# Row sums by transfers and VectorE, b2 in norm 1's shift, norm 3 on ScalarE, and all pieces in a new order

## The chip, the cores and the metric

The kernel runs on one core of one Trainium2 chip. A core has TensorE (PE in the profile; its weight loads are PEld), VectorE (DVE), ScalarE (ACT), GpSimd (POOL) and SyncE (SP), which issues transfers. Each engine takes its instructions in the order of the program; semaphores make one wait for another. Sixteen DMA engines move data. The metric is the device time in microseconds (us) of one execution.

## What is computed

32 graphs of 512 nodes with 256 features pass through two layers of masked attention with norms around them. Cut to what matters:

```python
# layer 0
allowed = (adj > 0) | (adj.swap > 0) | eye
scores  = where(allowed, (q * 32**-0.5) @ k.T, -inf)        # 8 heads of 32
x1  = layernorm1(x + (softmax(scores) @ v) @ Wo.T + bo)      # with gain and shift
ff  = relu(x1 @ W1.T + b1) @ W2.T + b2                       # 1024 hidden
x2  = layernorm(x + layernorm2(x1 + ff))                     # "norm 3" is the outer one
# layer 1
scores = where(adj == 0, -inf, q @ k.T / sqrt(32))
out = layernorm(x2 + (softmax(scores) @ v) @ Wo.T + bo)      # "norm 4"
```

## The kernel before

A graph's score matrix is held transposed, keys on the 128 partitions and queries along the row. One layer of one graph is cut into eight pieces k = 0 to 7: a group of four heads (`hg` = 0 or 1) and a block of 128 keys. For each piece, `scores` (L338) makes four matmuls of 32 rows into one PSUM tile of 128x2048, and ScalarE's exp turns it into `p` (L349). `masked` (L352) multiplies `p` by the 0/1 mask on VectorE. `product` (L356) multiplies with the values and adds over the four key blocks into `acc`; the last one is copied to `cT`. The exps aren't normalised, so their sums over all 512 keys are needed as divisors. The pool of `p` has eight buffers of 1 MB, those of the score tile and of `acc` one each, and the pool of small PSUM tiles three.

The divisors are made thus. `pair` (L374) issues an accumulating transfer p[k] += p[k+1] from GpSimd, for k = 0, 2 and 4. `fold` (L379) adds two `p` on VectorE (L381), three times a layer, so that p[2] holds the sum of the four blocks of head group 0 and p[3] that of group 1. `sums` (L392) sums over the 128 partitions: four matmuls with a block of ones, on TensorE (L402). `divide` (L410) turns blocks of 32x32 (L414), takes the reciprocal, spreads it back with another transpose (L420) and multiplies `cT` with it (L421); two small GpSimd additions keep a running total that tells at the end whether any sum left the range. For layer 1 of the last graph the sums are matmuls over all four blocks without pairs and folds.

`project` (L453) then multiplies `cT` with Wo. The norms work on quarters of 128 nodes: `residual_statistics` (L447) adds the residual to the PSUM result and takes mean and variance on VectorE; `root` (L433) forms (variance + eps)^-0.5 in two small GpSimd instructions (L436, L437); `affine` (L442) applies gain and shift on VectorE (L444, L445). Norm 3 is one VectorE instruction a quarter (L518); norm 4 is done by ScalarE (L532) with scale 1/sigma and bias -mean/sigma, which `offset` (L523) forms on VectorE. `hidden` (L472) and `mlp` (L498) are the two dense layers. `residual1` adds the row b2 to x1 for all nodes by an accumulating transfer (L169), after the transposes of x1 were taken for the hidden layer; `residual` and `residual2` add bov and norm 2's shift in the same way.

SyncE's queue loads x twice, the cast adjacency as `m0` and its transpose as `m1`, and transposes x for layer 0 by transfers (`flip`, `sort`).

Order: nothing is scheduled by a tool. The bodies of `opening`, `period` and `closing` are lists of such calls over up to five graphs in different stages, written out by hand under `manual_schedule`; each engine gets its instructions in that order. `period` runs for 29 graphs. A piece here is a method with all its engines' work: `scores` holds its exp, `out2` the addition and the statistics.

Of the kernel before, what the change touches and what calls it, by code (L numbers as in the profile page):

```python
# [9 lines left out]
F32 = mybir.dt.float32  # L10
# [8 lines left out]
EPS = 1e-5  # L19
# [8 lines left out]
def kernel(ctx: ExitStack, tc: tile.TileContext, t: dict, out: bass.AP):  # L28
# [88 lines left out]
    bo.append(spread("L1_gnn_bo"))  # L117

# [31 lines left out]
    def plain(pools: ExitStack):  # L150
# [6 lines left out]
        BEATS = ND * NQ  # L157
# [10 lines left out]
        def add_row(dst, row):  # L168
            nc.gpsimd.dma_start(out=dst, in_=row[:, None, :].to_broadcast([P, NQ, D]), accum_op=ALU.add)  # L169

        class Absent:


            def __getattr__(self, name):
                return lambda *args, **kw: None

        class Graph:


            def __init__(self, b):  # L180
                self.b = b
                self.mv, self.rs, self.pf, self.total = {}, {}, {}, {}

            def tile(self, tag, shape, dtype=F32, **kw):
                t = work.tile([P, *shape], dtype, tag=tag, name=f"{tag}_{self.b}", **kw)
                setattr(self, tag, t)
                return t


            def load(self):  # L190
                if not hasattr(self, "x"):
                    nc.sync.dma_start(out=self.tile("x", [NQ, D]), in_=x[self.b].rearrange("(c p) d -> p c d", p=P))

            def again(self):

                if not hasattr(self, "x1"):
                    nc.sync.dma_start(out=self.tile("x1", [NQ, D]), in_=x[self.b].rearrange("(c p) d -> p c d", p=P))

            def cast(self):

                if hasattr(self, "code"):
                    return
                self.code = hbm.tile([N, N], BF16, tag="code", name=f"code_{self.b}")
                nc.gpsimd.dma_start(
                    out=self.code.rearrange("(p c) k -> p (c k)", p=P),
                    in_=adj[self.b].rearrange("(p c) k -> p (c k)", p=P),
                )

            def entries(self):

                if hasattr(self, "m0"):
                    return
                nc.sync.dma_start(
                    out=self.tile("m0", [NQ, N], BF16), in_=self.code.rearrange("(c p) k -> p c k", p=P)
                )
                self.tile("m1", [NQ, N], BF16, bufs=3)
                for i in range(NQ):
                    nc.sync.dma_start_transpose(out=self.m1[:, i, :], in_=self.code[:, i * P : (i + 1) * P])

            def masks(self):  # L220

                nc.vector.tensor_tensor(self.m0, self.m0, self.m1, ALU.max)
                diagonal = self.m0.rearrange("p c (k q) -> p (c k) q", q=P)[:, :: NQ + 1, :]
                nc.vector.tensor_tensor(diagonal, diagonal, ident_b[:, None, :].to_broadcast([P, NQ, P]), ALU.max)
                nc.vector.tensor_scalar(self.m0, self.m0, 0.0, None, ALU.is_gt)
                nc.vector.tensor_scalar(self.m1, self.m1, 0.0, None, ALU.not_equal)
# [6 lines left out]
            def once(self):  # L233

                if self.b == 0:
                    value_bias(0)

            def once1(self):
                if self.b == 0:
                    value_bias(1)  # L240

            def residual(self):

                add_row(self.x1, bov[0])
                add_row(self.x, be2)

            def flip(self, n, i):


                if i == 0:
                    self.tile("v", [NQ, D])
                    self.tile("kT", [ND, N])
                if n > 0:
                    h, j = divmod(i, 2)
                    dst, src = self.flipped(n, h)[:, :, j * P : (j + 1) * P], getattr(self, f"x{n}")[:, i, :]
                    nc.sync.dma_start_transpose(out=dst, in_=src.bitcast(U16))
                elif self.b > 0:
                    src = x[self.b, i * 2 * P : (i + 1) * 2 * P, :]  # L260
                    nc.sync.dma_start_transpose(out=self.flipped(0, i), in_=src.bitcast(U16))

            def flipped(self, n, h):
                t = self.x2[:, :2, :] if n == 1 else self.v[:, 2 * h : 2 * h + 2, :]
                return t.rearrange("p c d -> p (c d)").bitcast(U16).rearrange("p (a q) -> p a q", q=2 * P)

            def sorted(self, n, h):
                t = self.x2[:, 2:, :].rearrange("p c d -> p (c d)") if n == 1 else self.kT[:, h, :]
                return t.bitcast(U16).rearrange("p (a q) -> p a q", q=2 * P)

            def sort(self, n, h):

                if n == 0 and self.b == 0:
                    return
                src, dst = self.flipped(n, h), self.sorted(n, h)
                for w in range(2):
                    for i in range(2):
                        nc.sync.dma_start(
                            out=dst[i * P // 2 : (i + 1) * P // 2, w * ND : (w + 1) * ND, :], in_=src[w::2, i::2, :]
                        )  # L280

            def join(self, n, h):
                if n == 0 and self.b == 0:

                    self.transpose(self.x, h)
                    return
                if h == 0:
                    self.tile("xT", [ND, N])
                words = self.xT.bitcast(U16).rearrange("p c (q w) -> p c q w", w=2)
                for w in range(2):  # L290
                    nc.scalar.copy(
                        words[:, :, h * 2 * P : (h + 1) * 2 * P, w], self.sorted(n, h)[:, w * ND : (w + 1) * ND, :]
                    )


            def transpose(self, src, h):

                if h == 0:
                    self.tile("xT", [ND, N])
                ps = ps_d.tile([P, ND, 2 * P], F32, tag="d", name=f"psT_{self.b}_{h}")  # L300
                for c in range(ND):
                    for j in range(2):
                        nc.tensor.transpose(
                            ps[:, c, j * P : (j + 1) * P], src[:, 2 * h + j, c * P : (c + 1) * P], ident
                        )
                nc.scalar.copy(self.xT[:, :, h * 2 * P : (h + 1) * 2 * P], ps)

            def value(self, layer, h):
                if h == 0 and layer != 0:
                    self.tile("v", [NQ, D])  # L310
                ps = ps_d.tile([P, 2, D], F32, tag="d", name=f"psV_{self.b}_{h}")
                for j in range(2):
                    at = slice((2 * h + j) * P, (2 * h + j + 1) * P)
                    for i in range(ND):
                        nc.tensor.matmul(
                            ps[:, j, :],
                            self.xT[:, i, at],
                            proj[layer][0][2][:, i, :],
                            start=(i == 0),
                            stop=(i == ND - 1),  # L320
                        )
                nc.scalar.copy(self.v[:, 2 * h : 2 * h + 2, :], ps)

            def query_key(self, layer, which, c, h=None):

                tag = ("qT", "kT")[which]
                dst = getattr(self, tag) if c or h or (which and layer == 0) else self.tile(tag, [ND, N])
                w, bias = proj[layer][0][which], proj[layer][1 + which]
                at = slice(0, N) if h is None else slice(h * 2 * P, (h + 1) * 2 * P)
                ps = ps_d.tile([P, at.stop - at.start], F32, tag="d", name=f"psQK_{self.b}_{which}_{c}_{h}")  # L330
                for i in range(ND):
                    nc.tensor.matmul(  # L332
                        ps, w[:, i, c * P : (c + 1) * P], self.xT[:, i, at], start=(i == 0), stop=(i == ND - 1)
                    )
# [3 lines left out]
            def scores(self, layer, k):  # L338
                if k == 0:
                    self.layer, self.p, self.acc = layer, {}, {}  # L340
                hg, kc = divmod(k, NQ)
                s = ps_s.tile([P, HPC, N], F32, tag="s", name=f"psS_{self.b}_{k}")
                for j in range(HPC):
                    at = slice(j * HD, (j + 1) * HD)
                    nc.tensor.matmul(  # L345
                        s[:, j, :], self.kT[at, hg, kc * P : (kc + 1) * P], self.qT[at, hg, :], start=True, stop=True
                    )
                p = work.tile([P, HPC, N], F32, tag="p", name=f"p_{self.b}_{k}", bufs=8)
                nc.scalar.activation(p, s, AF.Exp, scale=SCALE)  # L349
                self.p[k] = p  # L350

            def masked(self, layer, k):  # L352
                p, m = self.p[k], (self.m0, self.m1)[layer]
                nc.vector.tensor_tensor(p, p, m[:, k % NQ, None, :].to_broadcast([P, HPC, N]), ALU.mult)  # L354

            def product(self, k):  # L356
                hg, kc = divmod(k, NQ)
                if kc == 0:
                    self.acc[hg] = ps_a.tile([P, N], F32, tag="acc", name=f"psA_{self.b}_{hg}")
                for j in range(HPC):  # L360
                    h = hg * HPC + j
                    nc.tensor.matmul(  # L362
                        self.acc[hg][j * HD : (j + 1) * HD, :],
# [1053 lines left out]
```

## Time and profile before

| what | value |
|---|---|
| time, median of 3 runs (lowest, highest) | 3073.57 us (3073.37, 3074.45) |
| span of the profiled execution | 3072.4 us |
| HBM read and written | 89.01 MB and 33.55 MB, 40 GB/s over the span |
| DMA share of q0 (issued by GpSimd) and q1 (by SyncE) | 51.2% and 16.1% of the span |
| mean granted TensorE clock | 0.999 |
| p<-p accumulations, 1 MB each | 189, landing 7.7 us after the issue |
| kT<-v, 64 KB each | 248, landing 3.9 us after the issue |
| masking, 128x2048 | 512, 2279 ns each |
| fold, 128x2048 | 189, 2286 ns each |
| row-sum matmuls as recorded | 1072 records (two for each matmul) |

A row of a group names line, engine, operation, output and inputs by their names in the program (buffer numbers left out), shapes and count; then the busy time in us, the mean of one in ns, and the idle time of that engine just ahead of it with what ended it. In a timeline, each line has start, duration, and what ran. The share of a DMA engine is the time that its packets took; with several queues at work it can pass 1.

### The profile page before, as it was taken

How to read it: one execution, taken by the hardware profiler on the slowest of the kernel's cores; microseconds unless marked ns; L12 is line 12 of the kernel's file. 1: busy time of each engine (PE TensorE's matmuls, PEld its weight loads, DVE VectorE, ACT ScalarE, POOL GpSimd, SP SyncE). 2: the span in 40 equal slices, each digit the busy share in tenths (PEclk: the TensorE clock that was granted, in tenths of full speed). 3: DMA queues.
4: the chain of work that ended last, by engine and by line, in shares of the span. 5: the costliest groups of instructions: out<-in, count | busy, mean ns of one | idle time of the engine just before them, and what ended most of it. 6: DMA issues, size and time to landing. Idle time of an engine off the chain costs nothing. (4 is left out here: it accounts for less than half of the span.)

```text
span 3072.4 us, 44237 instructions
## 1 busy us (share of the span) xinstructions
PE 3049.0 (99%) x17218; PEld 1728.9 (56%) x17218; DVE 2648.1 (86%) x3458; ACT 1707.3 (56%) x1983; POOL 1039.0 (34%) x1254
## 2 busy tenths in 40 slices
PE   8999999999999999999999999999999999999998
PEld 4555655556555555555555555655556555555564
DVE  6798889888889888898888988889888889888887
ACT  5455565555556555565556655565555556555554
POOL 1333333433334332343323333333433334332332
PEclk9999999999999999999999999999999999999999
DMA  9876677666767666676666766667766767666543
GB/s 207 155 141 129 116 141 145 140 123 126 136 138 148 121 131 124 138 154 122 133 124 136 148 134 131 114 141 145 139 124 126 136 137 148 120 131 124 117 83 70
DMA packets 341064, 406.54 MB, mean 132 GB/s; under 512 B 149616, under 2 KB 315632, under 8 KB 316144
## 3 DMA queue, kind: packets, MB, share of 16 engines
q0 software_dynamic: 95824, 282.09, 51.2%
q1 hardware_dynamic: 245024, 121.56, 16.1%
q8 instruction: 137, 2.24, 0.3%
q14 instruction: 79, 0.65, 0.1%
HBM read 89.01 MB, written 33.55 MB: 40 GB/s over the span
## 5 line engine op out<-in xcount | busy, mean ns | idle before, releaser
L349 ACT ACTIVATE p<-psS 128x2048 f32<-128x2048 f32 x512 | 962.2, 1879 | 657.1 <-PE psS L345 655.4
L354 DVE TENSOR_TENSOR p<-p,m 128x2048 f32<-128x2048 f32 x512 | 1155.4, 2279 | 8.4 <-ACT p L349 8.2
L436 POOL TENSOR_SCALAR rs<-mv 128x2 f32<-128x2 f32 (+1 forms) x320 | 326.3, 1020 | 940.6 <-DVE mv L431 939.7
L345 PE MATMUL psS<-qT,kT 32*128 32x512 f32 x4096 | 583.9, 640 | 2.8 <-ACT p L349 1.3
L362 PE MATMUL psA<-p,v 128*32 128x512 f32 x4096 | 492.7, 598 | 0.9 <-ACT cT L372 0.7
L502 PE MATMUL psF<-w_L_gnn_W,hT 128*128 128x256 f32 x2048 | 468.5, 382 | 0.0
L481 PE MATMUL psH<-xT,w_L_gnn_W 128*128 128x256 f32 x2048 | 467.3, 384 | 0.7 <-DMA w_L_gnn_W<-in_L_gnn_W_dram 0.7
L502 PEld LDWEIGHTS psF<-w_L_gnn_W,hT 128*128 128x128 f32 x2048 | 383.8, 190 | 123.0 <-issue 76.4
L481 PEld LDWEIGHTS psH<-xT,w_L_gnn_W 128*128 128x128 f32 x2048 | 381.4, 190 | 120.3 <-issue 47.9
L381 DVE TENSOR_TENSOR p<-p,p 128x2048 f32<-128x2048 f32 x189 | 429.5, 2286 | 6.4 <-DMA p<-p 4.7
L345 PEld LDWEIGHTS psS<-qT,kT 32*128 32x128 f32 x4096 | 159.9, 182 | 300.5 <-issue 117.2
L437 POOL TENSOR_TENSOR rs<-rs,neg_half 128x2 f32<-128x2 f32 (+1 forms) x320 | 299.6, 936 | 26.8
L362 PEld LDWEIGHTS psA<-p,v 128*32 128x32 f32 x4096 | 109.9, 109 | 315.3 <-issue 234.5
L489 ACT ACTIVATE hT<-psH,c_L_gnn_b 128x256 f32<-128x256 f32 x512 | 215.2, 472 | 120.6 <-PE psH L481 117.3
L417 POOL TENSOR_TENSOR total<-total,sT 128x16 f32<-128x16 f32 x128 | 28.4, 222 | 732.0 <-DVE sT L414 732.0
L461 PE MATMUL psO<-w_L_gnn_Wo,cT 128*128 128x256 f32 x1024 | 241.0, 383 | 0.9 <-DVE cT L421 0.9
L332 PE MATMUL psQK_None<-xT,w_L_gnn_Wqkv 128*128 128x512 f32 x512 | 238.4, 598 | 2.4 <-DMA w_L_gnn_Wqkv<-in_L_gnn_Wqkv_dram 2.4
L372 ACT COPY cT<-psA 128x512 f32<-128x512 f32 x128 | 75.0, 586 | 280.7 <-PE psA L362 280.7
L377 POOL DMA_DIRECT2D p<-p x189 | 188.2, 996 | 117.8 <-PE psA L362 108.7
L449 DVE TENSOR_TENSOR y<-psF,x 128x256 f32<-128x256 f32 x128 | 53.9, 421 | 200.1 <-PE psF L502 197.6
L461 PEld LDWEIGHTS psO<-w_L_gnn_Wo,cT 128*128 128x128 f32 x1024 | 189.3, 190 | 52.0 <-DVE cT L421 23.0
L430 DVE BATCH_NORM_STATS2 st<-y 128x6 f32<-128x256 f32 x384 | 164.3, 428 | 13.1
(68 smaller groups left out, 2930.8 us busy)
## 6 DMA issues: line engine op xcount, KB each, us to landing
p<-p POOLq DMA_DIRECT2D x189, 1024.0 KB, 7.7
x<-in_x_dram SPq DMA_DIRECT2D x64, 512.0 KB, 5.1
x<-bov POOLq DMA_DIRECT2D x64, 512.0 KB, 9.2
code<-in_adj_dram POOLq DMA_DIRECT2D x32, 512.0 KB, 6.6
m<-code SPq DMA_DIRECT2D x32, 512.0 KB, 5.6
x<-s_L_gnn_ln_b POOLq DMA_DIRECT2D x32, 512.0 KB, 10.4
x<-s_L_gnn_b POOLq DMA_DIRECT2D x32, 512.0 KB, 5.4
out_dram<-x SPq DMA_DIRECT2D x32, 512.0 KB, 9.1
```

Of the source, the lines that this page charges most:

```text
L332: nc.tensor.matmul(ps, w[:, i, c * P : (c + 1) * P], self.xT[:, i, at], start=(i == 0), stop=(i == ND - 1))
L345: nc.tensor.matmul(s[:, j, :], self.kT[at, hg, kc * P : (kc + 1) * P], self.qT[at, hg, :], start=True, stop=True)
L349: nc.scalar.activation(p, s, AF.Exp, scale=SCALE)
L354: nc.vector.tensor_tensor(p, p, m[:, k % NQ, None, :].to_broadcast([P, HPC, N]), ALU.mult)
L362: nc.tensor.matmul(self.acc[hg][j * HD : (j + 1) * HD, :], self.v[:, kc, h * HD : (h + 1) * HD], self.p[k][:, j, :], start=(kc == 0), stop ...
L381: nc.vector.tensor_tensor(self.p[dst], self.p[a], self.p[b], ALU.add)
L436: nc.gpsimd.tensor_scalar(rs, self.mv[n][:, a:b, 1:2], EPS, None, ALU.add)
L437: nc.gpsimd.tensor_tensor(rs, rs, neg_half[:, a:b, None], ALU.pow)
L461: nc.tensor.matmul(ps[:, j, :], self.cT[:, k, at], wo[layer][:, k, :], start=(k == 0), stop=(k == ND - 1))
L481: nc.tensor.matmul(ps[:, j, :], w1[:, c, at], self.xT[:, c, h * 2 * P : (h + 1) * 2 * P], start=(c == 0), stop=(c == ND - 1),)
L489: nc.scalar.activation(self.hT[h][:, f + j, :], ps[:, j, :], AF.Relu, bias=b1[:, f + j : f + j + 1])
L502: nc.tensor.matmul(ps, self.hT[h][:, f, j * P : (j + 1) * P], w2[:, f, :], start=(f == 0), stop=(f == NF - 1))
```

## The change

Every piece is cut by engines: `scores` and `exp`, `hidden` and `relu`, `add`, `stats` and `aggregate`, `center` and `affine` are calls of their own, and `opening`, `period` and `closing` are new lists of these over five graphs, `period` for 26 graphs. New or different in what is computed where:

- Row sums: after the folds, two accumulating transfers from GpSimd (`halve`) add the upper 64 partitions of the sum to the lower 64, and then 32 to 32. Four transfers from SyncE (`spread`) put the four heads' 32x512 side by side on the partitions of `part`. VectorE transposes blocks of 32x32 (`blocks`) and adds 32 to one (`reduce`). Reciprocal, spreading back and the division stay. Layer 1 of the last graph keeps the matmuls.
- b2 is added to norm 1's shift once, so x1 holds it already; its effect on the hidden layer is taken from b1 (`hidden_bias`, 16 matmuls of one column, once). The transfer of `residual1` goes.
- Norm 3 is done by ScalarE like norm 4, with `offset` for its bias on VectorE.

```diff
-        def add_row(dst, row):
-            nc.gpsimd.dma_start(out=dst, in_=row[:, None, :].to_broadcast([P, NQ, D]), accum_op=ALU.add)
...
+        def hidden_bias():
+            ps = ps_d.tile([P, NF], F32, tag="d", name="psB_2")
+            for f in range(NF):
+                for c in range(ND):
+                    nc.tensor.matmul(
+                        ps[:, f : f + 1],
+                        w1[:, c, f * P : (f + 1) * P],
+                        b2_c[:, c : c + 1],
...
+            nc.vector.tensor_tensor(b1, b1, ps, ALU.subtract)
+            nc.vector.tensor_tensor(be1, be1, b2, ALU.add)
...
-            def sums(self, k, hg, first=False, last=False):
...
+            def halve(self, layer, hg, rows):
+                p = self.p(layer, 2 + hg)
+                nc.gpsimd.dma_start(out=p[:rows], in_=p[rows : 2 * rows], accum_op=ALU.add)
+
+            def spread(self, layer, hg, j):
+                part = self.at("part", (layer, hg), [N], bufs=1)
+                nc.sync.dma_start(out=part[j * HD : (j + 1) * HD, :], in_=self.p(layer, 2 + hg)[:HD, j, :])
...
+            def blocks(self, layer, hg):
+                src = self.dense("R", (1, hg), [N]) if self.final(layer) else self.at("part", (layer, hg), [N], bufs=1)
+                nc.vector.transpose(self.sT(layer, hg).rearrange("p a b -> p (a b)"), src)
+
+            def reduce(self, layer, hg):
+                if self.final(layer):
+                    nc.vector.tensor_copy(self.total(layer, hg), self.sT(layer, hg)[:, :, 0])
+                else:
+                    nc.vector.tensor_reduce(self.total(layer, hg), self.sT(layer, hg), AX.X, ALU.add)
...
-            def norm3(self, i):
-                mean, rs = self.mean(3, i), self.rs[3][:, i, :]
-                nc.vector.tensor_scalar(self.x2[:, i, :], self.y.pop(i), mean, rs, ALU.subtract, ALU.mult)
...
+            def norm(self, n, i):
+                nc.scalar.activation(
+                    self.x2[:, i, :], self.y(n, i), AF.Identity, bias=self.ms(n)[:, i, :], scale=self.rs(n)[:, i, :]
+                )
```

From the new `period`, in its order, what concerns the row sums of graph c in layer 0 and the pieces that follow roots directly (all else left out):

```python
c.fold(0, 2, 2, 0)
c.halve(0, 0, P // 2)
...
c.product(0, 4)
c.scores(0, 7)
...
c.pair(0, 4)
c.masked(0, 6)
...
c.halve(0, 0, P // 4)
c.spread(0, 0, 2)
...
c.masked(0, 7)
c.fold(0, 3, 6, 7)
c.fold(0, 3, 3, 4)
c.halve(0, 1, P // 2)
...
c.spread(0, 0, 0)
...
d.masks(0)
c.spread(0, 0, 3)
...
c.halve(0, 1, P // 4)
...
b.masked(1, 1)
...
c.spread(0, 0, 1)
...
b.masked(1, 0)
b.scores(1, 2)
b.exp(1, 2)
b.value_out(1, 0)
c.blocks(0, 0)
c.reduce(0, 0)
d.value(0, 0)
b.scores(1, 5)
b.exp(1, 5)
...
c.aggregate(1, 0)
c.root(1, 0, 2)
c.center(1, 1)
c.affine(1, 1)
...
c.aggregate(1, 2)
c.relu(0, 7)
c.root(1, 2, 4)
c.affine(1, 3)
...
c.aggregate(2, 0)
c.hidden(1, 2)
c.relu(1, 3)
c.root(2, 0, 2)
...
c.affine(2, 1)
```

The buffers of `p` are still eight. A buffer is free again when the last piece that reads it is done; for the two sums of a layer that is now the last `spread`. `part` has one buffer.

## The prediction

> **What bounds the kernel now.** I read the page first (engine shares, slices, chain), then the groups of instructions split by shape, then one steady graph in the table of windows and in the timeline of each engine, and last the waits.
>
> ```profile
> PE 3049.0 (99%) x17218; PEld 1728.9 (56%) x17218; DVE 2648.1 (86%) x3458; ACT 1707.3 (56%) x1983; POOL 1039.0 (34%) x1254
> PE   8999999999999999999999999999999999999998
> DMA  9876677666767666676666766667766767666543
> ...
> 1000.00:1095.00 95.00, 95.00 (x538) 53.92 (x537) 83.05 (x109) 53.51 (x63) 33.18 (x40) 1.00 0.69 134
> ```
>
> TensorE is busy in 3049.0 of 3072.4 us, and in the window (columns: length, then busy us of PE, PEld, DVE, ACT, POOL, clock, DMA share, GB/s) it has no gap at all. So a steady graph costs what TensorE's instructions cost. The casts of the adjacency, one a graph, start at 218.32 us and, 26 graphs later, at 2684.84 us: the period is 94.87 us. 32 periods make 3035.8 us; the 36.6 us left are filling and draining. The chain of waits covers only the last few us and bounds nothing before them. VectorE is second: 83.05 us busy in that window, and what its idle time is made of decides how much TensorE's saving is worth:
>
> ```profile
> L449 DVE TENSOR_TENSOR y<-psF,x 128x256 f32<-128x256 f32 x4 | 1.7, 422 | 6.5 <-PE psF L502 6.5
> L445 DVE SCALAR_TENSOR_TENSOR x<-cent,rs,s_L_gnn_ln_b 128x256 f32<-128x256 f32 x4 | 1.9, 485 | 1.1 <-POOL rs L437 0.9
> L445 DVE SCALAR_TENSOR_TENSOR z<-cent,rs,x 128x256 f32<-128x256 f32 x4 | 1.9, 484 | 1.2 <-POOL rs L437 0.9
> L518 DVE TENSOR_SCALAR x<-z,mv,rs 128x256 f32<-128x256 f32 x4 | 1.5, 403 | 1.1 <-POOL rs L437 1.1
> ```
>
> These are the groups of the same window (the figure after the second bar is the idle time before the group). 6.5 us go to TensorE, 2.9 us to GpSimd's roots, and 95.0 - 83.05 - 9.4 = 2.55 us are small gaps between instructions. Without the waits VectorE needs 85.6 us of a period of 94.87.
>
> What the row sums cost TensorE I take from start to start in its timeline, as busy times of neighbours overlap:
>
> ```profile
> 1014.88 1.06 PE L362 MATMUL psA<-p,v 128*32 128x512 f32 x8
> 1015.77 1.04 PE L402 MATMUL psR<-p,ones 128*32 128x512 f32 x8
> 1016.66 2.78 PE L362 MATMUL psA<-p,v 128*32 128x512 f32 x24
> ...
> 1033.53 1.06 PE L402 MATMUL psR<-p,ones 128*32 128x512 f32 x8
> 1034.42 1.04 PE L362 MATMUL psA<-p,v 128*32 128x512 f32 x8
> ...
> 1062.77 1.04 PE L402 MATMUL psR<-p,ones 128*32 128x512 f32 x8
> 1063.74 1.14 PE L345 MATMUL psS<-qT,kT 32*128 32x512 f32 x8
> ```
>
> 0.89, 0.89, 0.97, and 1.00 us for the fourth (1066.72 to 1067.72): mean 0.94, four times a graph.
>
> [...] Here every `p<-p` is in q0; in a stretch of two of them (1058 to 1060 us in the table of windows) the share is 1.02 at 209 GB/s, so some 210 GB/s fills all engines. [...]
>
> ```profile
> 1054.45 2.26 DVE L354 TENSOR_TENSOR p<-p,m 128x2048 f32<-128x2048 f32 x1
> ...
> 1054.63 2.16 POOL L436 TENSOR_SCALAR rs<-mv 128x2 f32<-128x2 f32 x1
> ```
>
> The root's first half takes 2.16 us and ends with the masking (1056.7); where VectorE waits it takes 0.35. So a slow root costs nothing by itself: VectorE is working then. [...]
>
> **The change part by part, per graph.**
>
> TensorE. The row sums leave (only the last graph's layer 1 keeps its 32 matmuls): 4 x 0.94 = -3.75 us, to 91.1. The 16 one-column matmuls of `hidden_bias` come once.
>
> VectorE. `reduce` is new, 4 a graph, 512 elements to 16. Nearest rows: the 512-element transpose at 0.71 us and multiply at 0.69; [...] I take 0.70 [...]: +2.8. Three more `offset` at 0.154: +0.5. Norm 3's four TENSOR_SCALAR at 0.403 leave: -1.6. `blocks` reads `part` in SBUF in place of PSUM; the transposes of either source take 0.70 to 0.71: 0. Masks, folds, adds and statistics keep number and shape. Sum 85.6 + 1.7 = 87.3 us.
>
> Waits of VectorE that the new order itself forces. A root as VectorE sees it is 1.3 us in the trace (aggregate ends 1016.09, next scale 1017.38). In the new stream `affine(1,3)` stands directly behind `aggregate(1,2)`, and `affine(2,1)` behind `aggregate(2,0)`: 1.3 each. `affine(1,1)` has one `center` of 0.47 before it: 0.8. `affine(2,2)` and `offset(3,2)` have 1 to 1.5 us of work before them: 0.3 each. Sum 4.0 (0 if GpSimd were instant, 7 if the roots also queue behind GpSimd's transfers): 91.3 us. Behind a waiting `affine` stand the maskings and folds, and behind those TensorE's products.
>
> ScalarE. Norm 3 adds 4 x 0.55 (row of norm 4) = 2.2 us to 53.5; exps wait for scores anyway. Hidden. Uncovered, 2.2.
>
> GpSimd. Eight accumulating `halve` at the 1.0 us of a `p<-p` issue, less b2's 1.3: 33.2 to 39.9 us of some 92. Hidden, but roots and pairs queue behind them (in the 7 above).
>
> SyncE. 16 `spread` more at about 1.0 us issue (four `kT<-v` take 4.08 us). Each waits for the halving, and the prefetches queued behind it wait too; those are wanted most of a period later. Hidden.
>
> DMA. Now 0.69 x 94.87 = 65.5 us. Halves: 4 x (0.52 + 0.26 MB) at 210 GB/s = +15. Spreads, 1.05 MB in 2 KB rows, like `kT<-v`: about +5 (2 to 10). b2's row no longer added: -2.5. Sum 83 of some 92 us, 0.90. Not the bound, but queues form. The tightest place: `halve(0,0,32)` stands behind `pair(0,4)` in GpSimd's queue, and that behind `product(0,4)`. One issue, 7.7 us landing of the pair (row `p<-p`), some 1.5 for the halving behind it, four spread issues of 1.0, landing 3.9 (row `kT<-v`): 18 us to `blocks(0,0)`. VectorE has beside it three maskings (6.7), two folds (4.5), masks (2.3), a fourth masking (2.2) and small ones (1.1): 16.8. 1.2 us of waiting stay. The buffers that `spread` holds longer: `exp(1,5)` takes that of `p(0,2)`; TensorE has 21 us (start to start) between `product(0,4)` and the end of `scores(1,5)`: covered by 3. The other three reuses have over 10 us.
>
> b2 in norm 1's shift and the removed row addition free only hidden work. The last graphs pay some latency in draining: +3.
>
> Sum: TensorE 91.1; VectorE 87.3 + 4.0 + 1.2 = 92.5. VectorE becomes the bound by a little. For 28 graphs 92.5, for four at the edges, where the table of windows shows VectorE at 31 to 35 of 40 us, 91.1; with filling and draining 36.6 + 3: 2590.0 + 364.4 + 39.6 = 2994. That is the profiled span; the median is 1.2 us above it: 2995.
>
> **Rivals.**
> (a) TensorE stays the only bound: the roots and transfers all hide. For: ordering by pieces (center apart from affine) gives room. Against: the two direct waits above. 32 x 91.1 + 39.6 = 2955.
> (b) The waits for psF stay too: half of the 6.5 us comes on top of 91.3, as mlp to norm 2 to the next transpose is a chain through both engines. 94.5: 28 x 94.5 + 404 = 3050.
> (c) Slower: the software DMA queue runs late. Place: `blocks(0,0)` at the head of VectorE, fed by pair, two halves and spread in one queue order. Price: at 0.90 load each of the four landings 1 to 1.5 us later, all of it VectorE's, as nothing there is slack: 92.5 + 4.2 = 96.7, 28 x 96.7 + 404 = 3112. It decides from 2.4 us of lag a graph on (94.9). For: the load. Against: the slices now hold stretches with a DMA share of 0.00 (1014 to 1022 us), so there is room to move into.
> (d) No change: the removed time comes back exactly, 94.8: 3072. That the change doesn't do what it says I exclude: the new program holds 32 row-sum matmuls in place of 536.
>
> **Numbers.** 0.2% is what a measurement of this kernel can tell from no change. Forecast (91.5 to 93.6 a graph, 2965 to 3025) 0.44; (a) 0.18; (b) 0.15; (c) 0.19; (d) 0.04. Faster 0.44 + 0.18 + 0.15 = 0.77, same 0.04, slower 0.19. The range leaves out most of (c) and the lowest edge of (a): 2945 to 3095.
>
> **What would show it.** Right: a period of 92 to 93 us; TensorE at 98 to 99% with small waits for VectorE; VectorE near 93% with its idle time put down to roots (4 us a graph) and `part` (1); DMA near 0.9; `reduce` at 0.6 to 0.75 us. Wrong: `blocks` waiting several us for `part` (c); long waits for psF (b); no waits of TensorE (a); exps waiting for a transfer, which I hold covered.

## The result, and the profile after

The changed kernel takes 3292.65 us (median of 4 runs, 3284.91 to 3302.06), the kernel before 3074.01 in the same comparison: ratio 1.0712, 95% interval 1.0692 to 1.0731. It is slower by 7%, and the time lies above the whole range that I gave. The profiled execution has a span of 3292.5 us.

The page of the kernel after (engine totals, DMA by slices of the span, DMA queues):

```profile
PE 3032.3 (92%) x16242; PEld 1758.3 (53%) x16242; DVE 2652.7 (81%) x3556; ACT 1760.1 (53%) x2111; POOL 1149.4 (35%) x1474
DMA  8898989998888998898988899888999888898862
q0 software_dynamic: 95056, 364.42, 65.5%
q1 hardware_dynamic: 269488, 154.63, 20.9%
```

No engine is near its span now. TensorE has given up its 99% for 92%, VectorE its 86% for 81%; only the DMA row has filled, from 6s and 7s to 8s and 9s. The casts, one a graph, lie at 334.54 and, 25 graphs later, at 2843.43 us: a period of 100.36 us. What lies outside 25 such periods (filling, draining, and seven graphs' worth of work) is 783.6 us; the kernel before has 94.86 and 701.0.

One steady graph in the table of windows, cut in two (length, busy us of PE, PEld, DVE, ACT, POOL, clock, DMA share, GB/s):

```profile
1035.00:1085.00 50.00, 49.85 (x278) 24.86 (x280) 46.69 (x62) 33.18 (x37) 17.67 (x26) 1.00 0.73 131
1085.00:1135.00 50.00, 44.19 (x234) 30.18 (x227) 36.40 (x51) 22.57 (x31) 18.80 (x22) 0.93 1.06 196
```

In the first half TensorE has no gap and the DMA engines seem to have room (0.73). In the second they are full from end to end (1.06), and TensorE loses 5.8 us. VectorE's timeline shows where (the bracket is the idle time before the instruction and what ended it):

```profile
1105.34 0.18 DVE L518 BATCH_NORM_AGGREGATE mv<-st_(2_1_7268 128x2 f32<-128x6 f32 x1
1105.56 0.48 DVE L534 SCALAR_TENSOR_TENSOR cent_(2_1_7274<-y_(2_1_7266,mv,s_L_gnn_ln_g 128x256 f32<-128x256 f32 x1
1115.20 0.71 DVE L471 STREAM_TRANSPOSE sT_(1_0_7283<-part_(1_0_7203 128x512 f32<-128x512 f32 x1 [9.16 <-DMA part_(1_0_7203<-p_(1_2_6956]
1115.95 0.69 DVE L477 TENSOR_REDUCE total_(1_0_7285<-sT_(1_0_7283 128x16 f32<-128x512 f32 x1
1116.74 0.25 DVE L480 RECIPROCAL r_(1_0_7296<-total_(1_0_7285 128x16 f32<-128x16 f32 x1
1116.91 0.36 DVE L512 TENSOR_TENSOR y_(2_0_7303<-psF,x 128x256 f32<-128x256 f32 x1
```

`blocks(1, 0)` (L471) stands at the head of VectorE's queue and waits 9.16 us for `part`. Behind it stands `add(2, 0)` (L512), which would free a PSUM tile. TensorE's timeline at that place:

```profile
1104.44 3.62 PE L571 MATMUL psF<-w_L_gnn_W,hT 128*128 128x256 f32 x16
1107.90 3.62 PE L555 MATMUL psH<-xT,w_L_gnn_W 128*128 128x256 f32 x16
1117.32 5.62 PE L555 MATMUL psH<-xT,w_L_gnn_W 128*128 128x256 f32 x16 [5.81 <-DVE y_(2_0_7303 L512]
```

`hidden` needs that tile, so TensorE stands for 5.81 us; then the same 16 matmuls take 5.62 us where they took 3.62. The window 1115 to 1120 us shows a clock of 0.50:

```profile
1115.00:1120.00 5.00, 2.68 (x6) 2.19 (x7) 3.44 (x8) 0.00 (x0) 1.34 (x4) 0.50 1.05 190
```

Cut finer, the table has 0.50 from the end of the wait (1117.3) to 1121 us, 0.90 in the next us and 1.00 from 1122 on. With the 2.0 us of slower matmuls the wait costs 7.8 us. At this place between 700 and 2300 us of the trace 15 waits for `y`, of 5.2 to 9.6 us, are each followed by 16 matmuls in 5.1 to 6.8 us.

Why `part` is late shows in the queues. GpSimd and SyncE in that stretch:

```profile
1086.57 0.88 POOL L438 DMA_DIRECT2D p_(1_2_6956<-p_(1_2_6956  x1
...
1093.73 0.88 POOL L438 DMA_DIRECT2D p_(1_2_6956<-p_(1_2_6956  x1 [2.47 <-DMA p_(1_2_6956<-p_(1_2_6956]
```

```profile
1086.38 5.98 SPq L336 DMA_TRANSPOSE v<-in_x_dram  x2
1097.85 0.69 SPq L341 DMA_DIRECT2D kT<-v  x1
1099.29 2.05 SPq L443 DMA_DIRECT2D part_(1_0_7203<-p_(1_2_6956  x2
1101.39 1.48 SPq L341 DMA_DIRECT2D kT<-v  x1
1102.91 4.46 SPq L443 DMA_DIRECT2D part_(1_0_7203<-p_(1_2_6956  x2
```

The fold ends at 1085.8; the first halving is issued at 1086.6, the second, which needs the first, at 1093.7; the spreads follow from 1099.3, and the last lands at 1115.1: 29.4 us from fold to use. VectorE comes to it 20.2 us after the fold. Transfers of that stretch by line, with KB and median us from issue to landing:

```profile
p_(1_2_6956<-p_(1_2_6956 POOLq DMA_DIRECT2D x1, 512.0 KB, 6.9
p_(1_2_6956<-p_(1_2_6956 POOLq DMA_DIRECT2D x1, 256.0 KB, 5.4
part_(1_0_7203<-p_(1_2_6956 SPq DMA_DIRECT2D x4, 64.0 KB, 6.8
v<-in_x_dram SPq DMA_TRANSPOSE x2, 8.7
```

Three readings are open at this point. Theory Q: SyncE's queue holds the spreads behind flips and sorts. Theory D: the DMA engines are full, so all lands late in any order. Theory P: the lateness costs so much only because `blocks(1, 0)` stands ahead of `add(2, 0)`. Besides, the new order might be slow by itself.

### The profile page after: what moved, and what is told of

It reads as the page before. It is cut to its first block, busy times and chain, and to the rows that moved or that the text cites. A ratio compares the mean times of both kernels' runs of the same rounds, so it can differ in the third digit from the quotient of the medians.

```text
span 3292.5 us, 43923 instructions
## 1 busy us (share of the span) xinstructions
PE 3032.3 (92%) x16242; PEld 1758.3 (53%) x16242; DVE 2652.7 (81%) x3556; ACT 1760.1 (53%) x2111; POOL 1149.4 (35%) x1474
## 4 chain that ended last, share of the span: by engine, by line
DVE 33%; PE 29%; DMA 16%; SPq 7%; issue 7%; ACT 5%; POOL 2%; DVEq 0%; POOLq 0%; ACTq 0%
SPq L443 5%; PE psF L571 4%; PE psQK_None L383 4%; PE psH L555 3%; PE psO L501 3%; PE psQK L383 3%; PE psV L371 2%; SPq L341 2%; POOL rs L524 1%; PE psT L358 1%; DVE mv L518 1%; POOL rs L523 1%; ACT x L544 1%; DVE x L541 1%; DVE cT L492 1%
## 5 line engine op out<-in xcount | busy, mean ns | idle before, releaser
L501 PEld LDWEIGHTS psO<-w_L_gnn_Wo,cT 128*128 128x128 f32 x1024 | 202.8, 202 | 84.1 <-DVE cT L492 36.6
L383 PEld LDWEIGHTS psQK_None<-xT,w_L_gnn_Wqkv 128*128 128x128 f32 x512 | 92.6, 191 | 133.8 <-issue 109.4
L371 PE MATMUL psV<-w_L_gnn_Wqkv,xT 128*128 128x256 f32 x512 | 127.4, 392 | 0.0
L358 PE MATMUL psT<-ident,x 128*128 128x128 f32 x520 | 89.6, 292 | 40.3 <-ACT x L544 33.0
L371 PE MATMUL psV<-w_L_gnn_Wv,xT 128*128 128x256 f32 x512 | 124.4, 386 | 0.0
L371 PEld LDWEIGHTS psV<-w_L_gnn_Wqkv,xT 128*128 128x128 f32 x512 | 92.2, 189 | 58.0 <-issue 25.2
L371 PEld LDWEIGHTS psV<-w_L_gnn_Wv,xT 128*128 128x128 f32 x512 | 92.5, 190 | 36.5 <-issue 26.5
L363 ACT COPY xT<-psT 128x512 f32<-128x512 f32 x130 | 75.1, 578 | 60.7 <-PE psT L358 60.7
L323 POOL DMA_DIRECT2D x<-bov x64 | 98.1, 1532 | 3.2 <-PE psT L358 2.1
L348 ACT COPY xT<-kT 128x512 uint16<-128x512 uint16 x124 | 94.2, 765 | 7.0 <-DMA kT<-v 4.7
L376 ACT COPY v<-psV 128x512 f32<-128x512 f32 x128 | 73.9, 581 | 11.7 <-PE psV L371 11.6
```

The source lines that it names most:

```text
L348: nc.scalar.copy(words[:, :, h * 2 * P : (h + 1) * 2 * P, w], self.sorted(h)[:, w * ND : (w + 1) * ND, :])
L358: nc.tensor.transpose(ps[:, c, j * P : (j + 1) * P], src[:, 2 * h + j, c * P : (c + 1) * P], ident)
L371: nc.tensor.matmul(ps[:, j, :], xT[:, i, at], proj[layer][0][2][:, i, :], start=(i == 0), stop=(i == ND - 1))
L383: nc.tensor.matmul(ps, w[:, i, c * P : (c + 1) * P], xT[:, i, at], start=(i == 0), stop=(i == ND - 1))
L501: nc.tensor.matmul(ps[:, j, :], self.cT(layer)[:, k, at], wo[layer][:, k, :], start=(k == 0), stop=(k == ND - 1))
```

## The experiments

Ratios are to the kernel before, with the 95% interval. Period and edges (what lies outside 25 periods) are worked out from the casts as above; "DMA" is the time of q0 and q1 over 32 graphs. Where a mean wait is named below, it is that of VectorE at this place over the graphs between 800 and 2500 us of the trace.

| run | ratio | period | edges | DMA, us a graph |
|---|---|---|---|---|
| kernel before | 1 | 94.86 | 701 | 64.6 |
| kernel after | 1.0712 (1.0692 to 1.0731) | 100.36 | 784 | 88.9 |
| e1 sorts behind | 1.0667 (1.0649 to 1.0685) | 99.97 | 780 | 88.3 |
| e2 blocks late | 1.0673 (1.0644 to 1.0702) | 100.38 | 781 | 88.3 |
| e3 less load | 1.0505 (1.0473 to 1.0538) | 97.98 | 784 | 82.2 |
| e4 all sums on TensorE | 1.0159 (1.0142 to 1.0176) | 95.18 | 742 | 62.9 |
| e5 biases early | 1.0650 (1.0617 to 1.0682) | 99.27 | 774 | 88.8 |
| e6 and flips late | 1.0725 (1.0686 to 1.0764) | 100.00 | 788 | 89.0 |
| e7 and blocks late | 1.0561 (1.0535 to 1.0588) | 97.45 | 784 | 86.5 |
| e8 layer 1 on TensorE | 1.0133 (1.0116 to 1.0150) | 93.34 | 781 | 76.0 |
| e9 before, one sum moved | 1.0185 (1.0171 to 1.0199) | 96.86 | 709 | 71.5 |
| e10 before, norm 3 and b2 | 1.0138 (1.0122 to 1.0153) | 95.27 | 738 | 60.9 |
| e11 quarter halves | 1.0128 (1.0086 to 1.0170) | 95.02 | 728 | 74.3 |
| e12 e8, edges on TensorE | 1.0007 (0.9998 to 1.0015) | 93.32 | 742 | 73.5 |
| e13 e12, but (1, 1) by transfer | 1.0254 (1.0236 to 1.0273) | 96.39 | 741 | 78.5 |
| e14 e12, but (1, 0) by transfer | 1.0063 (1.0041 to 1.0084) | 94.84 | 741 | 79.4 |
| e15 before, norm 3 | 1.0078 (1.0063 to 1.0093) | 95.27 | 712 | 64.6 |
| e16 e14, blocks late | 0.9922 (0.9909 to 0.9935) | 92.86 | 740 | 79.4 |
| e17 e16, biases early | 1.0066 (1.0053 to 1.0080) | 94.14 | 747 | 80.3 |

e9, e10 and e15 start from the kernel before, all others from the kernel after. Changes of order are made in `period` (in e6 and e7 with a few lines in `closing`); e4, e8 and e11 to e14 change methods, and so act in `opening` and `closing` too.

**e1: SyncE's order alone.**

```diff
-            e.sort(1, 0, 0)          # between the flips and the spreads
-            e.sort(0, 1, 0)
             b.spread(1, 0, 3)
+            e.sort(1, 0, 0)
+            e.sort(0, 1, 0)
```

> Only SyncE's order is changed in the steady stretch: the two sorts that stand between the transposing loads of x and the last spreads of layer 1's first part go behind those spreads; the load on the DMA engines stays. Theory Q (SyncE's queue order: spreads stuck behind sorts that wait): the wait of blocks(1,0) for part, 9.2 us in the steady graph, falls under 3 us, the period from 100.4 to about 94, the time to about 3090. Theory D (the 16 DMA engines are full from 1090 to 1120 us, so each halving and spread lands late in any order): only the 1.5 to 2 us between the issues go, the wait stays at 6 to 8 us, the time at 3230 to 3270. Theory P (the place of blocks ahead of add(2,0) on VectorE turns the lateness into TensorE time) says nothing against D here.

3281.85 us, some 11 us below the kernel after: the period gains 0.4 us. But the wait has moved. A graph of e1 on VectorE:

```profile
1207.88 0.71 DVE L471 STREAM_TRANSPOSE sT_(1_0_7959<-part_(1_0_7877 128x512 f32<-128x512 f32 x1 [4.94 <-DMA part_(1_0_7877<-p_(1_2_7632]
...
1222.81 0.71 DVE L471 STREAM_TRANSPOSE sT_(1_1_8042<-part_(1_1_8035 128x512 f32<-128x512 f32 x1 [5.85 <-DMA part_(1_1_8035<-p_(1_3_7605]
```

The mean wait at `blocks(1, 0)` falls from 9.2 us to 5.7, and that at `blocks(1, 1)` rises from 2.0 to 5.3. So neither theory's number came. SyncE's order does make `part(1, 0)` late by some 3.5 us, which Q says, but taking that away alone gains next to nothing, as the next consumer waits instead. Q is not the whole cause.

**e2: the place on VectorE alone.**

```diff
-            b.blocks(1, 0)           # ahead of c.add(2, 0)
-            b.reduce(1, 0)
-            b.invert(1, 0)
-            b.guard(1, 0, 0)
             d.masked(0, 4)           # behind add(2, 0) and affine(2, 1)
+            b.blocks(1, 0)
+            b.reduce(1, 0)
+            b.invert(1, 0)
+            b.guard(1, 0, 0)
```

> blocks(1,0), reduce, invert and GpSimd's guard for it are moved behind add(2,0), its statistics, affine(2,1) and the masking of p(0,4). Transfers and their order stay. Theory P: hidden(1,2) no longer waits 5.8 us for add(2,0) nor runs slowly after it (16 matmuls in 5.6 us in place of 3.6), so 7 to 8 us a graph come back: period 92 to 94, time 3020 to 3080, blocks waits 2 to 4 us at its new place. Theories Q and D alone (VectorE waits as long wherever blocks stands, as part lands at the same time and VectorE is the bound): period 97 or more, time above 3180.

3287.63 us: nothing. P in this form falls, and the trace shows how. VectorE in the run e2:

```profile
1116.73 0.71 DVE L471 STREAM_TRANSPOSE sT_(1_0_7333<-part_(1_0_7203 128x512 f32<-128x512 f32 x1 [1.74 <-DMA part_(1_0_7203<-p_(1_2_6956]
...
1127.11 0.71 DVE L471 STREAM_TRANSPOSE sT_(1_1_7366<-part_(1_1_7359 128x512 f32<-128x512 f32 x1 [6.22 <-DMA part_(1_1_7359<-p_(1_3_6929]
```

ScalarE, then TensorE, in the same run:

```profile
1123.45 0.76 ACT L348 COPY xT<-kT 128x512 uint16<-128x512 uint16 x1 [5.66 <-DMA kT<-v]
```

```profile
1118.92 1.13 PE L571 MATMUL psF<-w_L_gnn_W,hT 128*128 128x256 f32 x4
1124.60 8.71 PE L571 MATMUL psF<-w_L_gnn_W,hT 128*128 128x256 f32 x28 [4.55 <-ACT hT L565]
```

With the first wait gone, VectorE waits at the next `part`, and ScalarE stands 5.66 us at `join(1, 0)` (its copy of the sorted words into xT) for a late sort, with the relu that TensorE needs behind it. Three consumers of late transfers follow one another; taking the first away hands the wait to the next. That fits D, but transfers late for another reason would look the same here.

**e3: less to move.** `bias(2)` and `bias(0)` are left out of `period`, so that their constants are missing from x2 and x.

> Leaves out, in the steady stretch, the two row additions by transfer (b's bias(2) and c's bias(0), 1.0 MB on x2 and x), which stand among the halvings of layer 1; so residual rows miss a constant. Theory D: 1.0 MB less in the full stretch is some 5 us of all DMA engines at the 210 GB/s seen; halvings and spreads land 3 to 5 us earlier, the wait of blocks(1,0) falls from 9.2 to 4 to 6 us, the time to 3130 to 3200. Theory Q: the spreads stay stuck behind the sorts; wait 8 us or more, time 3260 or more.

3231.76 us: 61 us for 1.0 MB a graph. Inside neither theory's numbers: more than Q, less than D allowed. The load counts, but this is a quarter of the loss. At `blocks(1, 0)` VectorE no longer waits at all, where D allowed 4 to 6 us; it waits 6.9 us in the mean at `blocks(1, 1)` instead, so most of the wait has moved on here too.

**e4: the new order without the transfers of the row sums.** `halve` does nothing, `reduce` only copies a column, and at the last `spread` of a head group:

```diff
-                nc.sync.dma_start(out=part[j * HD : (j + 1) * HD, :], in_=self.p(layer, 2 + hg)[:HD, j, :])
+                    for i in range(HPC):
+                        nc.tensor.matmul(
+                            ps[i * HD : (i + 1) * HD, :], ones, self.p(layer, 2 + hg)[:, i, :], start=True, stop=True
+                        )
```

> The new order with the row sums put back on TensorE (four matmuls with ones on each folded tile, 0.94 us each as in the kernel before), no halvings, no spreads, a copy in place of the reduce. If the transfers of the row sums carry the whole loss (Q, D and P agree on that): no wait of blocks beyond 1 us, TensorE 91.1 + 3.75 = 94.9 us a graph, time 3060 to 3090, as the kernel before. If the new order itself is at fault: above 3130.

3123.57 us, above the 3060 to 3090 expected. The steady period is as foretold, 95.18 against 94.9. The rest is at the edges: 742 us against 701. The new `opening` and `closing`, with norm 3 and b2 as the change has them, cost 41 us without any transfer of a row sum.

**e5, e6, e7: moving load instead of removing it.** e6 adds to e5 that flips, sorts and joins come later, with `again` ahead of the sorts and `load` behind them; e7 is e6 with e2's move.

```diff
             c.bias(1)
+            b.bias(2)                # e5: both from the full half to the other
+            c.bias(0)
```

```diff
+            d.flip(0)                # e6: flips, sorts and joins a third of a period later
+            d.flip(1)
             d.entry(0)
```

> The two row additions bias(2) and bias(0), 1.0 MB, move from the stretch in which the DMA engines are full (1085 to 1135 us of the steady graph, mean share 1.04) to the lighter one (1035 to 1085, mean 0.73), directly behind bias(1) in GpSimd's order. Nothing is left out. Theory D2 (what counts is the load of the full half, with several consumers of late transfers one behind the other: blocks(1,0), join(1,0), blocks(1,1)): as good as leaving them out, which gave 3232: 3215 to 3250. Rival L (the load of the whole period counts, since it is 89 of 100 us): no gain, 3275 or more.

> As the kernel with the row additions early, and besides the two transposing loads of x (1.0 MB, 8.7 us to landing), their sorts and joins go to the next period's first third, for graphs 5 to 30; again() is issued before the sorts and load() behind them. Theory D2: another 1.0 MB and eight 64 KB copies out of the full half, so the wait of blocks(1,0) falls below 4 us and join(1,0) no longer holds ScalarE; 3120 to 3190. Rival L: no gain over the row additions alone. A third outcome: the joins, now close together ahead of value(0,0), hold ScalarE and TensorE there, 3230 or more.

> The same with blocks(1,0), reduce and invert behind add(2,0) and the masking of p(0,4), as tried before by itself. Theory D2: with join(1,0) out of the way the place of blocks now counts, so up to 4 us a graph more than without: 3050 to 3130. Rival: blocks(1,1) takes over the wait once more, and nothing is gained against the kernel without this move.

3268.68, 3293.24 and 3241.77 us. Moving 1.0 MB saves 24 us where leaving it out saved 61, and moving a second 1.0 MB gives that back. In all three `blocks(1, 0)` waits no longer. But `blocks(0, 1)` in the first half, which waits for nothing in the kernel after, waits 1.4, 3.2 and 2.3 us in the mean, and `blocks(1, 1)` 7.0, 5.2 and 3.1. So the first half, at a share of 0.73, has no real room either: its own consumer gets late. My theory that only the full half counts (D2) held in none of the three. e7 is 51 us better than e6, and e2's same edit gave nothing; in e2 `join(1, 0)` took the wait over, and here the joins hardly wait. Why the move helps in e7 isn't shown, since `blocks(1, 0)` has no wait in e6 that it could take away.

**e8 and e12: layer 1 back on TensorE; then the edges too.** As e4, for `layer == 1`; in e12 also for layer 0 of graphs 0 to 2 and 29 to 31, which `opening` and `closing` compute.

> Row sums of layer 1 on TensorE (8 matmuls, 2 x 0.94 us a graph), those of layer 0 by transfers as in the changed kernel: 1.6 MB of halvings and 0.5 MB of spreads leave the full half. Theory D2: no wait for part is left, TensorE 93.0 a graph, and 78 us of filling and draining as both kernels in the new order show: 32 x 93.0 + 78 = 3054, within 3040 to 3090. Rival L: half of the loss stays, some 3200.

> The kernel with layer 1's row sums on TensorE (3116), with layer 0's there too for the graphs that opening and closing compute (0 to 2 and 29 to 31). The steady graph stays at 93.3. If what it lost at the edges against the kernel with all row sums on TensorE (781 against 742 us outside 25 steady periods) is waiting for the transfers of the row sums: 3074 to 3086. If it is the order of opening and closing: 3105 or more.

e8: steady 93.34 us, as expected (93.0), in every graph, which sets aside rival L (the load of the whole period counts); but 3115.9 us in all, as its edges stay at 781. e12: 3076.6 us, edges 742, just what e4 has. So of the 83 us that the edges lost, some 40 are the row sums' transfers there, and 41 come with the new opening and closing and the small parts in them.

**e11: bytes or latency.** Every halving moves a quarter of its columns, so three quarters of a row sum's columns are left partial; a maximum against 0.001, one small VectorE instruction a row sum, keeps them off zero.

```diff
-                nc.gpsimd.dma_start(out=p[:rows], in_=p[rows : 2 * rows], accum_op=ALU.add)
+                nc.gpsimd.dma_start(
+                    out=p[:rows, :, : N // 4], in_=p[rows : 2 * rows, :, : N // 4], accum_op=ALU.add
+                )
```

> The changed kernel with every halving moving only a quarter of its columns (0.2 MB in place of 0.78 MB a row sum; the sums are partial, and a maximum against 0.001, 0.2 us of VectorE each, keeps them off zero). Order, waits and number of transfers stay. Load theory (the bytes of the halvings, 2.3 MB a graph less, keep the engines full and all landings late): period 93 to 95, 3060 to 3120. Latency theory (each row sum is a chain of fold, two halvings and a spread, whose fixed costs make it late): period 98 or more, above 3220.

3109.19 us: 183 us of the 219 lost come back with the order and the number of transfers unchanged. So bytes make most of the loss, and not the fixed costs of the chain. They act in two ways: the halvings themselves get shorter, and the others find more room. The traces show both. `part(1, 0)` has landed 16.6 us after its fold in place of 29.2 (medians); 3.8 of these 12.6 us are gained by the end of the second halving, the rest behind it, by spreads that didn't change. And `pair(0, 2)`, the same in all, lands 13 to 14 us after its issue, where it took 16 to 18 in the kernel after and 9 to 11 in e4. A mean wait of 4.1 us is left at `blocks(1, 1)`; whether it is latency or the pairs that move beside it isn't shown:

```profile
1054.61 0.71 DVE L473 STREAM_TRANSPOSE sT_(1_1_7407<-part_(1_1_7400 128x512 f32<-128x512 f32 x1 [4.41 <-DMA part_(1_1_7400<-p_(1_3_6967]
```

**e13, e14: which of layer 1's two.** e12, with one of the two left to transfers.

> The new order; on TensorE the row sum of layer 1's first half, and all of the graphs at the edges; by transfers layer 0's two and layer 1's second half. Load theory: one row sum by transfer, some 6.5 us of all DMA engines, fits into the second half of the period, and its 34 us from fold to use are enough: TensorE 92.4 a graph, edges 742: 3052, within 3045 to 3065, faster than both kernels. If the second half's transfers still come late: above 3080.

> The mirror of it: layer 1's second half on TensorE, its first half by transfers, so blocks(1,0) keeps its place 20 us behind its fold at the head of VectorE. Load theory alone: as the other, 3045 to 3065. Place theory (two halvings, four spreads in 20 us stay too slow beside pairs, loads and row additions): a wait of 3 to 6 us for part stays and goes on to TensorE, 3110 to 3190.

3152.12 and 3097.25 us: the reverse of what I expected. VectorE in e13:

```profile
1048.19 2.29 DVE L438 TENSOR_TENSOR p_(1_3_6893<-p_(1_3_6893,p_(1_4_7000 128x2048 f32<-128x2048 f32 x1
...
1060.07 0.71 DVE L488 STREAM_TRANSPOSE sT_(1_0_7245<-psR 128x512 f32<-128x512 f32 x1
...
1075.58 0.71 DVE L488 STREAM_TRANSPOSE sT_(1_1_7328<-part_(1_1_7321 128x512 f32<-128x512 f32 x1 [4.73 <-DMA part_(1_1_7321<-p_(1_3_6893]
```

I had counted 34 us from fold to use from the trace of the kernel after, but from the start of the first of two folds, where the halving waits for the end of the second (29.3 us), and 9 of them were the wait at `blocks(1, 0)`. With it gone VectorE arrives 20.4 us after the fold (1075.58 - 4.73 - 1050.48), and 25.1 are needed. In e14 periods of 93 and of 97 us stand side by side, though VectorE waits at `blocks(1, 0)` in nearly every graph, in 14 of 18 for 3.6 to 5.4 us. TensorE in two of them, where VectorE had waited 4.11 and 8.55 us:

```profile
1441.72 3.72 PE L572 MATMUL psH<-xT,w_L_gnn_W 128*128 128x256 f32 x16 [0.76 <-DVE y_(2_0_9961 L529]
...
2098.12 6.69 PE L572 MATMUL psH<-xT,w_L_gnn_W 128*128 128x256 f32 x16 [5.22 <-DVE y_(2_0_14679 L529]
```

Of the shorter wait 0.76 us come through to TensorE, and the 16 matmuls behind it take 3.72 us, which is what such a group takes without a wait (3.62 to 3.72 us in the kernel before); of the longer one 5.22 come through, and the 16 matmuls behind it take 6.69 us.

**e16, e17: the place, now with less load.** e16 is e14 with e2's move; e17 adds e5's.

> Layer 1's second row sum on TensorE, its first by transfer, edges on TensorE as before, and blocks(1,0), reduce and invert moved behind add(2,0), affine(2,1) and the masking of p(0,4), 7 us later on VectorE. Place theory: the wait goes, 92.5 a graph and 742 at the edges: 3045 to 3070. Load theory: another consumer takes the wait over, as in the fully loaded kernel: 3085 or more.

> The same, with bias(2) and bias(0) moved to the lighter stretch behind bias(1). If e16 still waits for the load: 20 us or more faster than it. If e16 is bound by TensorE: the same within 8 us.

e16: 3053.18 us, 0.8% faster than the kernel before (0.9922, 0.9909 to 0.9935). The wait at `blocks(1, 0)` is gone in all but one graph. Its steady graphs in the table of windows:

```profile
1000.00:1092.00 92.00, 91.85 (x513) 53.29 (x512) 82.82 (x112) 54.84 (x67) 32.26 (x44) 1.00 0.90 166
1092.00:1184.00 92.00, 91.85 (x513) 53.34 (x512) 82.54 (x112) 54.80 (x67) 32.17 (x44) 1.00 0.90 166
```

TensorE has no gap left and bounds again, with the DMA engines at 0.90. e17 loses 42 us against it: with the row additions moved, `part(0, 1)` comes 1.7 us late in the first half, and TensorE waits 1.0 us for the division at `project`. As in e5, moved load is only another late transfer.

**e9: the row sum alone, in the old order.** One of the four sums goes by transfers through a stretch where the DMA engines were little used (a share of 0.25 from 1005 to 1025 us of the kernel before); the other folds write to other buffers.

```diff
-            b.fold(2, 2, 0)
-            b.sums(2, 0, first=True, last=True)
-            b.divide(0)
+            b.fold(1, 2, 0)
+            b.halve(P // 2)
+            b.halve(P // 4)
+            b.spread()               # four transfers, from GpSimd
             a.divide(1)
+            a.divide_late()          # blocks, reduce, reciprocal, widen, divide
```

> The kernel before in its own order, with one of its four row sums a graph (layer 1, first half) taken off TensorE in the way of the change: two halvings and four spreads, all issued from GpSimd, in the stretch where its trace shows the DMA engines nearly idle (1005 to 1025 us of its steady graph, 26 to 105 GB/s), and divided 30 us after the fold. The other folds go to other buffers so that none is held longer. If row sums by transfer are cheap where the DMA engines have room (theory D2): TensorE 0.94 us less a graph, 29 graphs, 27 us: 3042 to 3052. If a halving costs TensorE or VectorE more than it frees in any place: 3074 or more.

3131.03 us, 57 slower, and no wait for `part` at all. TensorE in e9:

```profile
1030.51 1.07 PE L362 MATMUL psA<-p,v 128*32 128x512 f32 x8
1032.28 1.92 PE L362 MATMUL psA<-p,v 128*32 128x512 f32 x16 [0.71 <-ACT cT L372]
```

The 0.9 us of row-sum matmuls had stood between the last product of one head group and the first of the next, just as long as ScalarE needs to copy `acc` out: in the kernel before the matmuls run from 1015.77 us to the next product at 1016.66, the copy from 1016.02 to 1016.61. Without them TensorE waits 0.71 us there, and 1.3 us more in three places for VectorE (a sum of 2.0 of the 2.9 us by which the period misses 93.9). That the matmuls were cover is what the waits show; I didn't test it by putting other work there.

**e10, e15: the small parts alone, in the old order.** e15 replaces norm 3's instruction by an offset and a ScalarE activation; e10 adds the hidden bias and b2 in the shift, and drops the transfer of b2.

> The kernel before with the two small parts of the change alone: norm 3 on ScalarE behind an offset on VectorE, and b2 in norm 1's shift with the hidden bias corrected once. My prediction priced both at nothing while TensorE is the bound: 3066 to 3078. If ScalarE's place in the chain to the transposes of x2 matters: above 3085. If the psF waits or the freed transfer matter: below 3060.

> The kernel before with norm 3 alone on ScalarE, behind its offset on VectorE. If the steady 0.4 us a graph of the run with both small parts is norm 3's: some 13 us over the kernel before, 3084 to 3092. If it came from b2 in norm 1's shift: 3070 to 3078.

3117.32 and 3097.49 us. Norm 3 costs 23 us: 0.4 us a graph and 11 us at the edges. b2 costs 20 more, all at the edges, none in the steady graph. TensorE at the start of e10:

```profile
62.53 1.89 PE L476 MATMUL psO<-w_L_gnn_Wo,cT 128*128 128x256 f32 x8
74.29 6.96 PE L173 MATMUL psB<-c_L_gnn_b,w_L_gnn_W 128*128 128x1 f32 x32 [9.87 <-DMA c_L_gnn_b<-in_L_gnn_b_dram]
```

Where I put them, the 16 one-column matmuls (32 records) wait 9.87 us for their column and then take 6.96 us, and VectorE waits for both. That is a cost of my place for them: in e4, which has the change's own place, they follow without a gap and take 3.63 us.

## Why the prediction was wrong, point by point

The forecast was 92.5 us for a steady graph, and 3 x 92.5 + 4 x 91.1 + 39.6 = 681.5 us for what lies outside 25 of them. Measured: 100.36 and 783.6. The miss of 298 us is 25 x 7.86 = 196 in the steady stretch and 102 at the edges.

- **TensorE, 91.1.** Held. e16, with one row sum on TensorE, has 92.15 us a graph in its steady stretch; less 0.94 is 91.2. What took time in the kernel after, in the graph shown, are the 5.8 us of waiting and 2.0 us more of matmuls at a granted clock of 0.50, neither of which my sum had.
- **VectorE, 87.3 and 4.0 of root waits.** Held: `reduce` takes 0.69 us (0.70 taken), all durations together grow by 1.4 us a graph from trace to trace (1.7 taken; by overlaps the busy time grows by only 0.14), and the root waits of the steady graph are 0.94 + 1.17 + 1.15 + 0.27 = 3.5. That VectorE would bound by a little didn't show: in e16 TensorE does.
- **DMA, "Sum 83 of some 92 us, 0.90. Not the bound, but queues form."** The step that failed, first in a term: "Halves: 4 x (0.52 + 0.26 MB) at 210 GB/s = +15". From e4 to the kernel after, q0's time grows by 0.655 x 3292.5 / 32 - 0.458 x 3121.8 / 32 = 22.7 us a graph, where the halvings' 3.1 MB were put at 15; the spreads take 3.3 (5 taken). So 89, not 83. I took 210 GB/s from pairs over all 128 partitions, and a halving reads and writes 64 or 32; those took 22.7 us, at 137 GB/s. No run shows why their rate is lower than that of pairs. e16 runs without a gap at a share of 0.90 of 92 us, so a load like my 83 was carried there, where no consumer stands too near. Whether 89 could be isn't shown.
- **"The tightest place ... 18 us to blocks(0,0)."** The same step, in its second half. At `blocks(0,0)` there is no wait: in the median `part` has landed 22.3 us after the fold, and VectorE comes at 23.4. I worked the chain out for one of four places, with the landing of a 64 KB copy in the kernel before for a spread (3.9) and 1.5 for the second halving. At `blocks(1,0)` it measures 29.4 us from fold to use, and VectorE comes after 20.2: second halving 5.4 to land, spreads 6.8. And I priced a wait of VectorE as VectorE's alone; here it went through a PSUM tile to TensorE, and cost 2.0 us more by a clock of 0.50.
- **Rival (c).** The right kind (`blocks` at the head of VectorE, its transfers late), in the wrong place and half the size: 4.2 us against 7.9 a graph. I gave it 0.19 because the slices held stretches without transfers. e9 shows that such a stretch of the old order does take one row sum without a wait for `part`; the lighter half of the new order took no more (e5, e6, e17).
- **SyncE hidden.** No: its order makes `part(1, 0)` some 3.5 us later. Changing it gains 0.4 us a graph, as the wait moves on (e1).
- **Norm 3 hidden; b2 frees only hidden work.** Not in the old order: 0.4 us a graph, and 11 and some 20 us at the start and end (e15, e10). In the new order e16 has no gap in its steady graph, so there norm 3 is hidden.
- **Filling and draining, 36.6 + 3.** Wrong by 102 us less 20 for my cheaper graphs. I took `opening` and `closing` as given, though they were written anew: some 40 us by the row sums' transfers there (e8 to e12), 41 by the new order with norm 3 and b2 in it (e4, e12). How these 41 divide isn't shown: in the old order norm 3 alone costs 11 at the edges (e15).
- **exp(1,5) covered by 3 us.** Held: in the window shown it waits for its scores only.

What stays open: whether the wait left in e11 is latency or load; why e2's move helps in e7; how the 41 us at the edges divide; and which of VectorE's pieces in e9 are late, and why.

## What to carry to other kernels

Before work goes from an engine to transfers, add up the DMA time in the fullest stretch, not over the span, with the rate of transfers of that very shape (here 137 GB/s for halvings, 210 for pairs), and work out fold-to-use for every consumer against the work beside it. When a wait is removed and nothing is gained, look for the next consumer of a late transfer, and add up the waits of all of them: here the order of a queue or the place of one instruction gained next to nothing under the full load (e1, e2), and with one row sum fewer the same move gave 44 us (e14 to e16). And instructions taken off the busiest engine may have been cover for another engine's latency (0.71 us behind ScalarE's copy in e9); that is read from waits here, not tested.

## What the runs showed of the hardware that I hadn't expected

Accumulating halvings, 64 and 32 partitions high, took 22.7 us of all DMA engines for 3.1 MB, 137 GB/s, where pairs over all 128 partitions had filled the engines at 210 (a share of 1.02 at 209 GB/s, 1058 to 1060 us in the kernel before). In the kernel after the share goes up to 1.17 (1090 to 1100 us, at 192 GB/s); how much of the 22.7 us is such time above 1 isn't shown. From e4 to e8, where nothing waits for `part` in the steady graphs, q0's time grows by 11.6 us a graph for 1.57 MB, 136 GB/s: with less load the rate is the same. A DMA share of 0.90 stood beside no lost time at all in e16, and 0.89 beside 7.9 us a graph in the kernel after: here the share of a period doesn't tell if transfers are late. A gap of 5.8 us on TensorE costs 7.8 in the kernel after, as the clock granted behind it was 0.50 for some 4 us; in e14 one of 0.76 us costs no more than itself (16 matmuls in 3.72 us behind it).
